# A mixture-of-experts feed-forward: one set of transposes, rows scaled once, routing between the blocks of the shared experts

## The chip, the core and the metric

The kernel runs on one core of one Trainium2 chip. The time is device microseconds (us) of one execution, taken as the median of several runs; the profile is one more execution, recorded by the hardware profiler. The engines have their own instruction queues and work side by side: TensorE (PE, with its weight loads shown apart as PEld), VectorE (DVE), ScalarE (ACT), GpSimd (POOL) and SyncE (SP), which here issues most of the DMA transfers. An engine executes its own instructions in order and waits on semaphores for the others.

## What is computed

A small Perceiver-like network of two layers on x of shape (4, 256, 256): 1024 tokens of 256 features, all in f32. Each block adds to x what it computes from the layer norm of x:

```python
x = x + L0_xattn(layernorm(x), ctx_1024, ctx_1024)
x = x + L0_attn(layernorm(x), pos, ...)
x = x + L0_ffn(layernorm(x), ...)
x = x + L1_xattn(layernorm(x), ctx_1024, mask)
x = x + L1_attn(layernorm(x), ...)
x = x + L1_ffn(layernorm(x), ...)
```

The change is in the third block (and moves some of its loads into the second). With u the normed rows:

```python
def L0_ffn(u, g_shared, W1_s, b1_s, W2_s, b2_s, g_routed, W1_r, b1_r, W2_r, b2_r, centroids):
    # _experts_mlp(x, g, W1, b1, W2, b2): for each expert
    #     gelu((rmsnorm(x) * g) @ W1 + b1) @ W2 + b2        (erf gelu, hidden size 1024)
    h_s = _experts_mlp(u, g_shared, W1_s, b1_s, W2_s, b2_s).sum(axis=-2)   # 2 shared experts
    scores = sigmoid(u @ centroids)                                        # 8 routed experts
    gpk, i_topk = top_k(scores, 2)
    gk = gpk / scores.sum(axis=-1, keepdims=True)
    h_r = weighted sum of the 2 chosen experts' outputs, weights gk
    return u + h_s + h_r
```

So the block's result is x + u + h_s + h_r. The router works on u, the experts on the rows of u divided by their root mean square.

## The kernel before

Tokens lie in 8 tiles of 128 (TT = 8, P = 128), the features in two halves of 128 (DC = 2), the hidden size in 8 parts of 128 (FC = 8). x stays in SBUF as [128, 8, 256]. Matmuls go through `contract` (L169, the matmul itself is L175), so most of them carry one line number in the profile and are told apart by the names of their tiles.

The blocks run one after the other (`BLOCKS`, L1644). `l0_attn` (L549) loads its weights, computes a relative-position attention over the batch axis, and ends with the output projection `ao`: a contraction over two halves and a bias row for each token tile, then an add to x on DVE (L668). Of its loads the ones named here are `a0_wT`, `a0_pT`, `a0_bias` and the row `a0_ob`, which the projection adds.

`l0_ffn` (L772) does the following. Where nothing else is said, the order on each engine is chosen by the tile scheduler from the dependences; the text order below is the program's.

- It loads the centroids and the output biases `f0_b2` (L781, L782), zeroes a DRAM table of rows, `f0_rows` (L785), and loads the first shared expert's weights (two loads of 1 MB, L797 to L803).
- `normed` (L233) computes the layer norm of all eight tiles into u (tile `xn`): statistics, `rsqrt` (twelve small DVE instructions, three Newton steps, L177 to L194), and one DVE instruction for each tile (L247).
- `transposed` (L255) turns u into `uT` by 16 PE transposes (tile `tr`) and four copies out of PSUM. The router's logits `cs` are contractions of `uT` with the centroids (L806 to L812); Exp (L814), a few DVE steps and `top2` (L817) give the chosen experts, the gates follow (L822).
- A second `rsqrt` gives the inverse root mean square r (L824). For each tile POOL adds u to x (L826) and DVE scales u by r (L827). A second set of 16 transposes with four scaled copies makes `sT`, the experts' input (L828).
- `place` (L694) works out where each token's row goes in a table sorted by expert: two matmuls for ranks (L707, L708), a chain of DVE instructions, and one large POOL product, `part` (L765, tile tag `h`), with its reduction (L769) for the biases of the routed tiles. Sixteen indirect DMAs on POOL's queue scatter the rows into `f0_rows` (L830 to L835).
- For each token tile the gates are transposed (`gT`, L839), copied by ACT (L841), multiplied with the biases (L843) and added to x (L844). Below this is the bias block.
- The eight routed experts' weights (16 loads of 1 MB) are issued on SP (L850 to L858).
- The shared experts (L845 to L872): for each of two experts e and each of four blocks n of 256 tokens, first the hidden layer `h`: eight parts f of 128 hidden units, each a contraction over two halves into half of a PSUM bank, and a Gelu from there into the SBUF tile `h` (two buffers). Two parts share a bank tile, and four such tiles rotate (`sc=(4, 1)`). Then the output `eo`: for each of two token tiles a contraction over eight f, and an add to x on DVE (L872).

```python
for f in range(FC):
    if f % 2 == 0:
        sc = self.sc_tile("h")[:, 0, :]
    part = sc[:, f % 2 * 256 : (f % 2 + 1) * 256]
    self.contract(part, [(w1[:, k, f * P : (f + 1) * P], sT[:, k, cols]) for k in range(DC)])
    nc.scalar.activation(h[:, f, :], part, AF.Gelu, bias=self.col("f0_b1", (NE + e) * FC + f))
```

- The routed experts (L873 to L936) work through 23 tiles of sorted rows in an order written out by hand (`manual_schedule`): rows are read back from `f0_rows`, transposed (`rT`), multiplied with the weights of the tile's expert, and written to DRAM; then the rows are gathered back and added to x with their gates (L937 to L946).

Inside `manual_schedule` the scheduler leaves the program's order as it is on every engine. The PSUM pools of the block are `mm_tile` (three banks), `sc_tile` (four) and `ps_o` (one).

Of the kernel before, what the change touches and what calls it, by code (L numbers as in the profile page):

```python
# [74 lines left out]
class Net:  # L75
# [157 lines left out]
    def normed(self, x, out, tiles=range(TT), square=None):  # L233
# [9 lines left out]
        if square is not None:  # L243
            nc.vector.tensor_mul(square, rstd, rstd)
            nc.vector.tensor_mul(square, square, mv[:, :, 1])
# [300 lines left out]
    def l0_attn(self, x):  # L546
# [3 lines left out]
        with ExitStack() as ctx:  # L550
# [6 lines left out]
            nc.sync.dma_start(bias, a["a0_bias"].partition_broadcast(P))  # L557

# [212 lines left out]

    def l0_ffn(self, x):  # L772
# [4 lines left out]
        with ExitStack() as ctx:  # L777
            pool = self.block(ctx, "f0", sc=(4, 1))
            rows = self.tc.dram_tile([SLOT_TILES * P, D], F32, name="f0_rows")
            results = self.tc.dram_tile([SLOT_TILES * P, D], F32, name="f0_results")  # L780
            cent = self.load_w(pool, "f0_cent")  # L781
            b2 = self.load(pool, "f0_b2", [NE + 2, D], a["f0_b2"])  # L782
            zero = pool.tile([P, D], F32, name="f0_zero")
            nc.gpsimd.memset(zero, 0.0)
            nc.sync.dma_start(  # L785
                rows.rearrange("(t p) d -> p t d", p=P), zero.unsqueeze(1).to_broadcast([P, SLOT_TILES, D])
            )
# [3 lines left out]
            ms = self.small.tile([P, TT], F32, tag="ms", name=self.name("ms"))  # L791
            u = self.normed(x, self.tokens("xn"), square=ms)
            w1_all, w2_all = (pool.tile([P, NE, DC * FF], F32, name=f"f0_w{n}_all") for n in (1, 2))
            with self.tc.tile_pool(name="f0_shared", bufs=1, reuse_waits="tile") as first:
                weights = {}

                def shared_weights(e):  # L797
                    weights[e] = (
                        self.load(first, "w1", [P, DC, FF], a["f0_W1_s"][e].rearrange("(k p) n -> p k n", p=P)),
                        self.load(first, "w2", [P, FC, D], a["f0_W2_s"][e].rearrange("(k p) n -> p k n", p=P)),  # L800
                    )

                shared_weights(0)  # L803
                uT = self.transposed(u, "xT", pool=first)
                score = first.tile([P, TT, NE], F32, name="f0_score")
                ps = self.mm_tile("cs")  # L806
                for i in range(TT):
                    self.contract(
                        ps[:, i * NE : (i + 1) * NE], [(uT[:, k, i * P : (i + 1) * P], cent[:, k, :]) for k in range(DC)]
                    )  # L810
# [34 lines left out]
                for e in range(2):  # L845
                    if e:
                        shared_weights(e)
# [799 lines left out]
def build(tc, a, out):  # L1647
    nc = tc.nc
    with ExitStack() as ctx:
# [4 lines left out]
        for block in BLOCKS:  # L1654
            x = getattr(net, block)(x)
# [163 lines left out]
```

## Time and profile before

| what | us |
|---|---|
| runs | 2363.99, 2364.1, 2373.08 |
| median of the runs | 2364.1 |
| the profiled execution | 2370.56 |
| its span in the profile | 2368.8 |
| its mean granted TensorE clock | 0.95 |

By stages, from the windows of the profile (a stretch from the span's start, and the busy time of two engines in it, in us):

| stretch | what runs there | length | PE busy | DVE busy |
|---|---|---|---|---|
| 0 to 270.0 | first cross attention, and the loads of the next blocks | 270.0 | 240.1 | 87.8 |
| 270.0 to 360.3 | `l0_attn` to its last `ao` matmul | 90.3 | 73.4 | 60.7 |
| 360.3 to 402.7 | norm, routing, transposes, bias block, first `h` parts | 42.4 | 30.6 | 32.7 |
| 402.7 to 511.1 | shared experts | 108.4 | 108.4 | 7.4 |
| 511.1 to 697.0 | routed experts | 185.9 | 184.8 | 39.8 |
| 697.0 to 2368.8 | gather, and the three blocks of layer 1 | 1671.8 | 1587.1 | 960.6 |

How to read such a profile: a share of busy time is an average over stages with different limits, so the stage that a change touches is read by itself. A line with "x32" stands for 32 records taken together; a 128x128 by 128x256 matmul in f32 leaves two records, so one part f of an `h` block (two matmuls) leaves four and a whole block 32. "[0.16 <-ACT h L867]" after a line means that the engine stood idle for 0.16 us before it, and that the wait ended with ACT's instruction of line 867 on tile `h`. The granted clock is a share of full speed. SPq is SP's DMA queue.

### The profile page before, as it was taken

What the parts mean: (1) busy time and instruction counts of PE and PEld (TensorE: products, weight loads), DVE (VectorE), ACT (ScalarE), POOL (GpSimd) and SP (SyncE); (2) the same over time, 40 slices, a digit from 0 to 9 for tenths busy, and PEclk for the clock granted to TensorE, in tenths of its full rate; (3) what the DMA queues carried; (4) which work ended last, traced back from release to release, by engine and by line L of the source; (5) the groups of instructions that cost most, each with busy time, mean ns of one, the idle gap of its engine ahead of it and who ended that gap; (6) DMA issues with size and microseconds to landing.
All of it is one profiled execution on the core that took longest, in us unless ns stands there. A gap on an engine that the chain in (4) does not pass through costs nothing.

```text
span 2368.8 us, 45856 instructions
## 1 busy us (share of the span) xinstructions
PE 2224.3 (94%) x19148; PEld 1339.5 (57%) x19148; DVE 1189.0 (50%) x2494; ACT 982.6 (41%) x1942; POOL 146.5 (6%) x270
## 2 busy tenths in 40 slices
PE   6999877999988999999999999999999899999996
PEld 4677535876752454455545554455554566666552
DVE  2333476012215766666666666665665176343545
ACT  0111111223333366655666556655555524344321
POOL 0000002100011000000000000000000042000121
PEclk9999866999999999999999999999999999999977
DMA  6121118101124112211121112210000120000000
GB/s 202 54 89 32 36 51 293 63 16 36 32 87 147 45 39 66 66 31 35 49 64 56 32 34 61 63 46 29 29 7 2 62 78 1 1 1 1 6 0 14
DMA packets 82432, 121.50 MB, mean 51 GB/s; under 512 B 5466, under 2 KB 52338, under 8 KB 82226
## 3 DMA queue, kind: packets, MB, share of 16 engines
q1 hardware_dynamic: 80690, 114.38, 15.4%
q0 software_dynamic: 1536, 4.20, 0.5%
q8 instruction: 151, 2.47, 0.4%
q14 instruction: 55, 0.45, 0.1%
HBM read 109.32 MB, written 9.24 MB: 50 GB/s over the span
## 4 chain that ended last, share of the span: by engine, by line
PE 87%; DVE 6%; issue 3%; ACT 2%; DMA 2%; SPq 0%; POOL 0%; POOLq 0%; DVEq 0%; ACTq 0%
PE sc L1092 14%; PE acc L1143 10%; PE mx L1105 9%; PE h L175 8%; PE v L1000 5%; PE k L1000 5%; PE ro L175 4%; PE we L175 3%; PE gram L414 2%; PE eo L175 2%; PE po L175 2%; PE sc L1560 2%; PE q L175 2%; PE xo L175 1%; PE qkv L175 1%
## 5 line engine op out<-in xcount | busy, mean ns | idle before, releaser
L1134 DVE TENSOR_REDUCE mx<-mx 128x1 f32<-128x512 f32 x988 | 636.6, 686 | 365.0 <-PE mx L1105 361.0
L1130 ACT ACTIVATE probs<-sc 128x512 f32<-128x512 f32 x988 | 536.8, 597 | 422.2 <-PE mx L1105 394.9
L1092 PE MATMUL sc<-qm,kT 32*128 32x256 f32 x3952 | 581.3, 401 | 8.9 <-ACT probs L1130 8.9
L1105 PE MATMUL mx<-kT,x_q 32*128 32x512 f32 x1976 | 561.1, 639 | 0.0
L1092 PEld LDWEIGHTS sc<-qm,kT 32*128 32x128 f32 x3952 | 352.3, 184 | 255.0 <-ACT probs L1130 129.3
L1143 PE MATMUL acc<-probs,v 128*32 128x256 f32 x4096 | 275.6, 386 | 0.0
L1143 PEld LDWEIGHTS acc<-probs,v 128*32 128x32 f32 x4096 | 107.3, 109 | 134.9 <-issue 90.1
L1105 PEld LDWEIGHTS mx<-kT,x_q 32*128 32x128 f32 x1976 | 150.9, 183 | 8.5 <-issue 7.2
L1000 PE MATMUL k<-slab,x_wk 128*32 128x512 f32 x1024 | 136.1, 618 | 11.8 <-DMA slab<-in_ctxT 10.9
L1000 PE MATMUL v<-x_wv,slab 128*32 128x256 f32 x2048 | 137.1, 385 | 0.0
L1574 DVE TENSOR_REDUCE negm<-mx 128x2 f32<-128x512 f32 x128 | 82.7, 686 | 94.8 <-PE mx L1566 92.9
L1572 ACT ACTIVATE probs<-sc 128x512 f32<-128x512 f32 x128 | 69.5, 595 | 136.1 <-PE mx L1566 93.9
L1566 PE MATMUL mx<-k,q 32*128 32x256 f32 x512 | 90.3, 435 | 24.5 <-DVE negm L1574 19.5
L309 ACT ACTIVATE kT<-k,cols 128x512 f32<-128x512 f32 x128 | 92.8, 783 | 23.2 <-PE k L1000 23.2
L346 POOL COPY wide<-rec 128x256 f32<-128x256 f32 x48 | 19.1, 398 | 1328.4 <-DVE rec L344 1317.0
L1000 PEld LDWEIGHTS v<-x_wv,slab 128*32 128x32 f32 x2048 | 53.4, 109 | 74.4 <-issue 46.3
L414 PE MATMUL gram<-x_ctx 128*128 128x257 f32 x256 | 79.2, 391 | 14.3 <-DMA x_ctx<-in_ctx 14.3
L1560 PE MATMUL sc<-qm,k 32*128 32x256 f32 x512 | 88.6, 439 | 0.0
L175 PE MATMUL h<-f_w_all,rT 128*128 x184 | 83.0, 594 | 0.7 <-DVE rT L888 0.6
L175 PE MATMUL ro<-f_w_all,hT 128*128 x368 | 83.3, 379 | 0.1
L912 ACT ACTIVATE hT<-hT,place 128x128 f32<-128x128 f32 x184 | 49.9, 383 | 77.8 <-PE hT L909 77.7
L175 PEld LDWEIGHTS ro<-f_w_all,hT 128*128 128x128 f32 x368 | 68.2, 190 | 9.1 <-issue 0.5
(365 smaller groups left out, 2664.4 us busy)
## 6 DMA issues: line engine op xcount, KB each, us to landing
slab<-in_ctxT SPq DMA_DIRECT2D x96, 512.0 KB
x_ctx<-in_ctx SPq DMA_DIRECT2D x16, 1024.0 KB
f_w_all<-in_f_W_r SPq DMA_DIRECT2D x16, 1024.0 KB
w<-in_f_W_s SPq DMA_DIRECT2D x4, 1024.0 KB
f_rows<-f_zero SPq DMA_DIRECT2D x1, 2944.0 KB
row<-f_rows SPq DMA_DIRECT2D x23, 128.0 KB
f_results<-y SPq DMA_DIRECT2D x23, 128.0 KB
kT<-away SPq DMA_DIRECT2D x128, 8.0 KB
```

The costliest lines, as they stand in the source:

```text
L175: nc.tensor.matmul(out, w, m, start=i == 0, stop=i == len(pairs) - 1)
L309: nc.scalar.activation(dst, ps, AF.Identity, bias=b, scale=own)
L414: nc.tensor.matmul(ps[:, : D + 1], t[:, :P], t, start=n == 0, stop=False)
L1000: nc.tensor.matmul(out[own], w[:, own], m, start=start, stop=not start, tile_position=(0, 32 * j))
L1092: nc.tensor.matmul(into[:, c * S : (c + 1) * S], kT[b, u, at // HALF][rows, at % HALF : at % HALF + P], qm[un][rows, :], start=True, stop= ...
L1105: nc.tensor.matmul(into, q[rows, b, u, t * P : (t + 1) * P], kT[b, u, at // HALF][rows, at % HALF : at % HALF + SLAB], start=True, stop=True,)
L1130: nc.scalar.activation(probs[j], sc[j], AF.Exp, scale=0.25)
L1134: nc.vector.tensor_reduce(mx[un2][:, k2 % 2, j, k2 // 2 : k2 // 2 + 1], bd[j], AX.X, ALU.max)
L1143: nc.tensor.matmul(acc[32 * j : 32 * j + 32, :S], v[b, chunk // VC][:, at : at + 32], probs[j][:, c * S : (c + 1) * S], start=k == 0 and c ...
L1560: nc.tensor.matmul(sc[j][:, c * S : (c + 1) * S], k[key][on_rows(j), u, c * P : (c + 1) * P], qm[i][on_rows(j), :], start=True, stop=True,)
L1566: nc.tensor.matmul(bd[j][:, c * S : (c + 1) * S], q[key][on_rows(j), u, c * P : (c + 1) * P], k[key][on_rows(j), u, :], start=True, stop=True,
L1574: nc.vector.tensor_reduce(negm[i2 % 2][:, :, 32 * j + UNIT_MAX[i2 % 2]], bd[j].rearrange("p (t s) -> p t s", s=S), AX.X, ALU.max, negate=True,
```

## The change

Four things are changed in the third block, and the order of its middle part is written out.

- The loads of the centroids, `f0_b2` and the first shared expert, and the zeroing of `f0_rows` move into `l0_attn`, after its own weight loads (`before_ffn`); their tiles live in a pool that is opened before `l0_attn`.
- The norm is done in two halves, tiles 0, 2, 4, 6 and then 1, 3, 5, 7. Both inverse roots are worked out first, and one DVE instruction for each tile writes u already divided by its root mean square (`by` = rstd times r). One set of transposes feeds both `uT` (plain copy, DVE) and `sT` (scaled by the gain, ACT). The logits of these scaled rows are multiplied back by `back`, which is one over r. x + u is computed by ACT as x times (1 + rstd) plus a shift, in place of POOL's adds.
- The routed experts' loads are issued ahead of the shared experts' first block.
- From Exp on, the order is by hand: `lower` (an `h` block) and `upper` (an `eo` block) alternate, with the gates, `place`, the scatter and the bias block at written places among them. `b2` gets the bank of `ps_o`, `gT` three buffers; the second shared expert is loaded after the first one's last block.

```diff
-    def normed(self, x, out, tiles=range(TT), square=None):
+    def normed(self, x, out, tiles=range(TT)):
...
-        if square is not None:
-            nc.vector.tensor_mul(square, rstd, rstd)
-            nc.vector.tensor_mul(square, square, mv[:, :, 1])
...
             nc.sync.dma_start(bias, a["a0_bias"].partition_broadcast(P))
+            self.before_ffn()
...
+    def before_ffn(self):
+        nc, a = self.nc, self.a
+        self.f0_rows = self.tc.dram_tile([SLOT_TILES * P, D], F32, name="f0_rows")
+        zero = self.early.tile([P, D], F32, name="f0_zero")
+        nc.gpsimd.memset(zero, 0.0)
+        self.f0_cent = self.load_w(self.early, "f0_cent")
+        self.f0_b2 = self.load(self.early, "f0_b2", [NE + 2, D], a["f0_b2"])
+        self.f0_shared = {}
+        self.shared_weights(0)
+        nc.sync.dma_start(
+            self.f0_rows.rearrange("(t p) d -> p t d", p=P), zero.unsqueeze(1).to_broadcast([P, SLOT_TILES, D])
+        )
+    def shared_weights(self, e):
+        a = self.a
+        self.f0_shared[e] = (
+            self.load(self.early, "w1", [P, DC, FF], a["f0_W1_s"][e].rearrange("(k p) n -> p k n", p=P)),
+            self.load(self.early, "w2", [P, FC, D], a["f0_W2_s"][e].rearrange("(k p) n -> p k n", p=P)),
+        )
...
-            ms = self.small.tile([P, TT], F32, tag="ms", name=self.name("ms"))
-            u = self.normed(x, self.tokens("xn"), square=ms)
+
+            back = pool.tile([P, TT], F32, name="f0_back")
...
-                shared_weights(0)
-                uT = self.transposed(u, "xT", pool=first)
+                sT = first.tile([P, DC, NT], F32, name="f0_sT")
+                uT = first.tile([P, DC, NT], F32, tag="h", name="f0_uT", bufs=2)
+                ps_c = self.mm_tile("cs")
+                logit = first.tile([P, TT, NE], F32, name="f0_logit")
+                columns = lambda t, c, half: t.rearrange("p c (t f n) -> p c t f n", f=2, n=P)[:, c, :, half, :]
+                for half in range(2):
+                    tiles = range(half, TT, 2)
+                    n = len(tiles)
+                    new = lambda what, *more: self.small.tile([P, n, *more], F32, tag=what, name=self.name(what))
+                    stats, mv = new("bn", 6), new("mv", 2)
+                    for k, i in enumerate(tiles):
+                        nc.vector.bn_stats(stats[:, k, :], x[:, i, :])
+                        nc.vector.bn_aggr(mv[:, k, :], stats[:, k, :])
+                    rstd = self.rsqrt(mv[:, :, 1], EPS)
+                    ms, by, keep, shift = new("ms"), new("by"), new("keep"), new("shift")
+                    nc.vector.tensor_mul(ms, rstd, rstd)
+                    nc.vector.tensor_mul(ms, ms, mv[:, :, 1])
+                    r = self.rsqrt(ms, EPS_RMS)
+                    nc.vector.tensor_mul(by, rstd, r)
+                    for k, i in enumerate(tiles):
+                        nc.vector.tensor_scalar(
+                            u[:, i, :], x[:, i, :], mv[:, k, 0:1], by[:, k : k + 1], ALU.subtract, ALU.mult
+                        )
+                    nc.vector.scalar_tensor_tensor(back[:, half::2], ms, EPS_RMS, r, op0=ALU.add, op1=ALU.mult)
+                    nc.vector.tensor_scalar(keep, rstd, 1.0, None, ALU.add)
+                    nc.vector.scalar_tensor_tensor(shift, mv[:, :, 0], -1.0, rstd, op0=ALU.mult, op1=ALU.mult)
+                    for c in range(DC):
+                        ps = self.mm_tile("tr")
+                        for k, i in enumerate(tiles):
+                            nc.tensor.transpose(ps[:, k * P : (k + 1) * P], u[:, i, c * P : (c + 1) * P], self.ident)
+                        ps = ps.rearrange("p (t n) -> p t n", n=P)
+                        nc.vector.tensor_copy(columns(uT, c, half), ps)
+                        nc.scalar.activation(columns(sT, c, half), ps, AF.Identity, scale=self.col("f0_gs", c))
+                    for i in tiles:
+                        self.contract(
+                            ps_c[:, i * NE : (i + 1) * NE],
+                            [(uT[:, k, i * P : (i + 1) * P], cent[:, k, :]) for k in range(DC)],
+                        )
+                    for k, i in enumerate(tiles):
+                        nc.scalar.activation(
+                            x[:, i, :], x[:, i, :], AF.Identity, bias=shift[:, k : k + 1], scale=keep[:, k : k + 1]
+                        )
+                nc.vector.tensor_tensor(
+                    logit, ps_c[:, : TT * NE].rearrange("p (t e) -> p t e", e=NE),
+                    back.unsqueeze(2).to_broadcast([P, TT, NE]), ALU.mult,
+                )
...
-                r = self.rsqrt(ms, EPS_RMS)
-                for i in range(TT):
-                    nc.gpsimd.tensor_add(x[:, i, :], x[:, i, :], u[:, i, :])
-                    nc.vector.tensor_scalar(u[:, i, :], u[:, i, :], r[:, i : i + 1], None, ALU.mult)
-                sT = self.transposed(u, "xT", "f0_gs", pool=first)
...
+                hidden = {}
+                def lower(e, n):
+                    w1 = self.f0_shared[e][0]
+                    cols = slice(n * 256, (n + 1) * 256)
+                    h = hidden[e, n] = first.tile([P, FC, 256], F32, tag="h", name=self.name("h"), bufs=2)
+                    for f in range(FC):
+                        if f % 2 == 0:
+                            sc = self.sc_tile("h")[:, 0, :]
+                        part = sc[:, f % 2 * 256 : (f % 2 + 1) * 256]
+                        self.contract(part, [(w1[:, k, f * P : (f + 1) * P], sT[:, k, cols]) for k in range(DC)])
+                        nc.scalar.activation(h[:, f, :], part, AF.Gelu, bias=self.col("f0_b1", (NE + e) * FC + f))
+                def upper(e, n):
+                    w2, h = self.f0_shared[e][1], hidden.pop((e, n))
+                    for q in range(2):
+                        i = 2 * n + q
+                        ps = self.mm_tile("eo")
+                        self.contract(ps[:, :D], [(h[:, f, q * P : (q + 1) * P], w2[:, f, :]) for f in range(FC)])
+                        nc.vector.tensor_add(x[:, i, :], ps[:, :D], x[:, i, :])
+                with self.tc.manual_schedule():
+                    nc.scalar.activation(score, logit, AF.Exp, scale=-1.0)
+                    lower(0, 0)
+                    nc.vector.tensor_scalar(score, score, 1.0, None, ALU.add)
+                    nc.vector.reciprocal(score, score)
+                    nc.vector.tensor_copy(chosen, self.top2(score, logit, first))
+                    nc.vector.tensor_reduce(total, score, AX.X, ALU.add)
+                    nc.vector.reciprocal(total, total)
+                    nc.vector.tensor_mul(score, score, chosen)
+                    nc.vector.tensor_mul(gates[:, :, :NE], score, total.unsqueeze(2).to_broadcast([P, TT, NE]))
+                    lower(0, 1)
+                    upper(0, 0)
+                    lower(0, 2)
+                    slots, shares, where, bias = self.place(first, pool, chosen, gates[:, :, :NE])
+                    upper(0, 1)
+                    for side in range(2):
+                        for i in range(TT):
+                            nc.gpsimd.indirect_dma_start(
+                                out=rows, out_offset=bass.IndirectOffsetOnAxis(ap=slots[:, side, i : i + 1], axis=0),
+                                in_=u[:, i, :], in_offset=None,
+                            )
+                    upper(0, 2)
+                    lower(0, 3)
+                    upper(0, 3)
+                    self.shared_weights(1)
                     for i in range(TT):
+                        ps = self.mm_tile("gT")
+                        nc.tensor.transpose(ps[: NE + 2, :P], gates[:, i, :], self.ident)
+                        gT = self.small.tile([NE + 2, P], F32, tag="gT", name=self.name("gT"), bufs=3)
+                        nc.scalar.copy(gT, ps[: NE + 2, :P])
+                        ps = self.ps_o.tile([P, 512], F32, tag="o", name=self.name("b2"))
+                        nc.tensor.matmul(ps[:, :D], gT, b2, start=True, stop=True)
+                        nc.vector.tensor_add(x[:, i, :], ps[:, :D], x[:, i, :])
+                    lower(1, 0)
                     for n in range(4):
+                        if n < 3:
+                            lower(1, n + 1)
+                        upper(1, n)
...
-        for block in BLOCKS:
-            x = getattr(net, block)(x)
+        x = net.l0_xattn(x)
+        with ExitStack() as ffn:
+            net.early = ffn.enter_context(tc.tile_pool(name="f0_early", bufs=1, reuse_waits="tile"))
+            x = net.l0_attn(x)
+            x = net.l0_ffn(x)
```

The lines of top two, gates, `place` and the loads of the routed weights are the same as before, apart from their place.

## Prediction

> **What bounds the kernel now.** I read the page from the top (busy time, clock, the chain that ended last), then stage windows, and then the chain and the timeline of the one stage that the change rewrites.
>
> ```profile
> span 2368.8 us, 45856 instructions
> PE 2224.3 (94%) x19148; PEld 1339.5 (57%) x19148; DVE 1189.0 (50%) x2494; ACT 982.6 (41%) x1942; POOL 146.5 (6%) x270
> ...
> PE 87%; DVE 6%; issue 3%; ACT 2%; DMA 2%; SPq 0%; POOL 0%; POOLq 0%; DVEq 0%; ACTq 0%
> ```
>
> TensorE sets the end. Work taken from another engine gains only where PE stands and waits for it. The windows (span's stretch, its length, then busy time of PE, PEld, DVE, ACT, POOL, the granted clock, DMA share, GB/s) show where that is:
>
> ```profile
> 360.30:402.70 42.40, 30.56 (x111) 20.54 (x111) 32.66 (x109) 6.18 (x16) 11.66 (x11) 0.60 1.02 363
> 402.70:511.10 108.40, 108.40 (x494) 93.55 (x495) 7.43 (x17) 28.40 (x60) 13.79 (x15) 0.99 0.17 57
> ```
>
> From the last `ao` matmul (360.3) on, PE waits for norms and routing, at a clock of 0.60. From 402.7 the shared experts run with PE busy for 108.40 of 108.40 us at 0.99. The chain of waits:
>
> ```profile
> 364.40 4.87 DVE xn L247 x7
> ...
> 370.64 6.64 PE cs L175 x32
> ...
> 383.08 3.90 PE tr L263 x16
> ...
> 407.50 6.91 PE eo L175 x32
> 414.40 6.91 PE h L175 x32
> ```
>
> One 256-token half of an expert layer is one block of 32 records: 6.92 us, whether `h` or `eo`, so 1.73 us for each of the four bank tiles of an `h` block, 0.865 for each of a tile's two f parts. Sixteen blocks make 16 x 6.92 = 110.7 us. The routed stage begins at 511.1, so the experts began as if at 511.1 - 110.7 = 400.4, with the bias work (L839 to L844) between the first `h` parts. The timeline of one `h` block shows the hand-over between TensorE and the Gelu:
>
> ```profile
> 455.52 1.70 PEld L175 LDWEIGHTS h<-xT,w 128*128 128x128 f32 x8
> 455.74 7.10 PE L175 MATMUL h<-xT,w 128*128 128x256 f32 x32
> ...
> 456.86 0.47 ACT L867 ACTIVATE h<-h,cols 128x256 f32<-128x256 f32 x1 [7.36 <-PE h L175]
> 457.39 5.04 PEld L175 LDWEIGHTS h<-xT,w 128*128 128x128 f32 x24 [0.16 <-ACT h L867]
> ```
>
> Eight loads are two parts (four records each). The third part's load then waits for the Gelu of the first, 456.86 + 0.47 = 457.33, and starts 0.06 later, 1.65 after the block's first matmul. The first two parts' matmuls last until 455.74 + 1.73 = 457.47, so today the wait is just covered.
>
> **The change, part by part.** All is counted from 360.3, where the last `ao` matmul ends in both.
>
> *Removed and hidden.* The 16 second transposes (3.90 above), their four scaled evacuations, eight POOL adds and eight scales L827 go. Eight ACTIVATEs (`keep`) come; by the 0.595 us of a 128x256 ACTIVATE they take 4.8 us on ACT beside DVE's norm. The loads moved ahead (`f0_cent`, `f0_b2`, `w1`, `w2`, the zeroing) go on SP in front of `a0_ob`, which is first needed at 336, and were landed at 259 already; POOL's memset comes before `bias`, which waits 204 us for its DMA. I cost them at nothing; if that cover failed, `ao` at 336 would start late by what is missing. The routed weights keep their start (after the last `ao`) and their queue; the second shared set, each half of it 1 MB that arrived within some 6 us before (449 to 455 and 456 to 461), is issued after the last reader of the first (`lower(0, 3)`, `upper(0, 3)`) and has the bias block and more to arrive in. The row scatter (POOL) starts after `part`, about 431 by the sum below, and 16 x 2.67 us (one start to the next, 413.51 to 416.18) ends at 474; it is needed at the routed stage, 60 us later. Instructions from the routed stage on are the same.
>
> *Front.* In the built program's instruction order the first half's small operations stand between the adds of the last four `ao` tiles. DVE then needs 2.07 to 2.27 us per tile (add 0.44, statistics 0.44 + 0.19, five or six small ones of 0.2) where `ao` tiles come every 1.68: the last add starts 1.35 late, at 361.65. It, four small ones and the last statistics reach 363.5; four `xn` of 0.33 follow with transposes behind them (eight of 0.25 at half clock), two `uT` copies of 0.68: 367.3. The second half's chain stands after these: 26 small ones of 0.2 = 5.2, to 372.5; four `xn` 1.3; transposes and `uT`, to 375.4; seven `cs` contractions of 0.43: 378.4; logit and Exp 0.9, to 379.3; the table load for Gelu (1.28, now behind Exp) and the first Gelu: 381.2, when PE goes on with tile 0's second part. A tile up to there costs 1.65, so the experts begin as if at 379.6: **-20.8 us**. Bounds: 376 (no backlog) to 383.
>
> *The wait inside a tile.* Now the order is by hand: `lower` writes part 0, its Gelu, part 1, its Gelu. In the built program part 1's first matmul waits, in all 32 bank tiles, for the Gelu of part 0 of the same tile: four tiles rotate, but each is guarded as a whole. Before, the scheduler had put another tile's part 0 between (the eight loads above). PE issues in order; the next tile's part 0, `eo` and the rank matmuls are queued behind. A tile becomes 1.65 (first matmul to part 1's load), 0.11 for that load with nothing over it (512.04 to 512.15 at the routed stage's first `h`, where the load after two starts at 512.58, one matmul of 0.43 later), and 0.865: 2.625 against 1.73. 32 x 0.895 = **+28.6**. Bounds: 1.60 (the block of 414.24 has its first Gelu after 1.07, not 1.12) and no load, 0.735, to 1.65 with a whole load of 0.21 (455.52 to 455.74), 0.995: 23.5 to 31.8.
>
> *Bias block.* `gT`, its copy, `b2` were laid between `h` parts and are now alone, PE waiting for ACT each time: 0.27 + 0.06 + 0.25 + 0.06 + 0.62 = 1.26 per token tile (389.10 to 390.36); at half clock a cycle took 1.92 (397.73 to 399.65). 8 x 1.26 = 10.1 to 15.4; half cold, **+12.7**.
>
> *Stall in `upper(0, 2)`.* `part` takes a buffer of `h` and so waits for `upper(0, 1)`. Then POOL 3.91, the reduce 1.67, and behind it on DVE the add (0.42) that frees the bank of `upper(0, 2)`'s second `eo`: 6.1 after `upper(0, 1)`, where PE is ready after 3.46. **+2.7** (0 to 4.4). The two rank matmuls, now in PE's order between blocks, took 0.32 + 0.43 (L707, L708); bare loads and a bank to wait for bring it to **+1.2** (0.75 to 1.5).
>
> *Clock.* `cs` and the bias block keep PE partly idle, and such stretches were granted half:
>
> ```profile
> 396.00:400.00 4.00, 3.60 (x8) 1.17 (x6) 3.56 (x9) 1.91 (x4) 3.55 (x2) 0.50 1.05 380
> ...
> 720.00:725.00 5.00, 3.30 (x32) 0.69 (x23) 1.79 (x6) 3.19 (x5) 3.48 (x8) 1.00 0.92 280
> 725.00:730.00 5.00, 3.46 (x32) 0.99 (x32) 1.49 (x4) 2.31 (x4) 0.47 (x5) 1.00 0.97 347
> ```
>
> The clock changed in steps of some 3.4 us, so after each of the two stretches one to two of them run cold. A tile takes 4.46 then (worked out at the rivals) against 2.625: 1.5 x 3.4 x (1 - 2.625 / 4.46) = 2.1, twice: **+4.2** (0 to 5.6, two steps each). Within `lower`, PE works 1.73 of 2.625 us, 66%; the last two rows are 66% and 69% and kept the full clock. I take no throttling there.
>
> A rule speaks against that: the Trainium skill, "TensorE: Matmul & The Clock Gate", section "A second HAM failure mode: psum-queue depth-cycling", says that micro-idles between groups of matmuls, with PSUM banks cycled, make the clock swing between half and full. By it the lowers would be the throttled rival below; by the two rows at 720 and 725 they are not, and the rows decide my sum.
>
> **Sum.** -20.8 + 28.6 + 12.7 + 2.7 + 1.2 + 4.2 = +28.6 us: the routed stage starts at 540. The profiled execution (2370.6, its span and 1.8 around it) would become 2399; it lay 6.5 over the median of the runs, and from that, 2364.1, the time is **2393**. All lower bounds (376, 23.5, 10.1, 0, 0.75, 0) give +10, all upper ones (383, 31.8, 15.4, 4.4, 1.5, 5.6) +41: 2374 to 2405.
>
> **The rivals.** *The clock stays at half in the lowers.* For: 0.50 at 396 to 400 with gaps of the same kind. Against: 720 to 730. At half clock both parts and a bare load double: 1.73 + 0.25 + 0.47 + 0.06 + 0.22 + 1.73 = 4.46, 1.84 more. The first two lowers cold: 8 x 1.84 less the step counted = +12.6, 2405; the same again after the bias block, 2418; all 32, 2393 + 58.9 - 4.2 = 2448. Chance 0.14.
>
> *The pause in the tile is not there (not slower).* If PE gets on with part 1 under the Gelu after all, the 28.6 fall away and the rest is 0: 2364; with the bias block warm and neither stall nor cold steps (-9.5) 2355. For: today 32 tiles run without a gap. Against: the row at 457.39, where one part fewer ahead of it would already have left PE idle, and the new order. It decides below a pause of 0.37 us per tile (11.8 us in all); between 0.37 and 0.6 the loss is small. Chance 0.13.
>
> *A transfer is late.* A half of the second shared set that nothing covers costs its 6 us: 2399. For: it can't be issued before the last reader of the first set, as now. Against: 12.7 us of that block and `upper(0, 3)`, 6.9, lie between. Chance 0.05. *The routing stays exposed as now*, so that the front's 20.8 isn't got: 2414; `cs` and what precedes it would have to take 40 us with half the transposes gone. Chance 0.02.
>
> **How the numbers follow.** My forecast has 0.66: 2393, its own range 2383 to 2401. This kernel tells a change from none from about 0.5% on, 11.8 us. Below 2352.3 only the no-pause rival with some further luck comes: faster 0.04; up to 2375.9 most of that rival and the low end of mine: same 0.12; slower 0.84. The range leaves out most of the no-pause rival and the colder half of the clock's: 2377 to 2409.
>
> **What would show it.** Right: 32 gaps of about 0.75 us on PE's weight loads, released by the Gelu's ACT, and `h` blocks of about 10.5 us against `eo` blocks of 6.9; Exp near 379; a bias block of 10 to 15 us on its own; the scatter over by about 475; the first `rT` matmul near 540; a span near 2397. Wrong: `h` blocks of 6.9 us; a granted clock of 0.5 in lowers after the first; `h` of expert 1 waiting for `w`; gaps at the routed stage for `f_rows`; or a difference that arises outside 360 to 540.

## The result, and the profile after

The changed kernel is slower: 2405.26 us, the median of four runs (2394.86 to 2406.04), against 2368.59 for the kernel before (four runs, 2363.99 to 2379.55). The ratio is 1.013, with a 95% interval of 1.0108 to 1.0152. That is 26 to 36 us. The ratios given here and below are those on record; the plain quotients of the medians differ from them by up to 0.0025 (here it is 1.0155), which changes no sign. One of e1's ten runs took 3581.77 us at a mean clock of 0.55 and is left out of its ratio.

The page of the changed kernel begins like this (busy time by engine, then the chain that ended last by engine):

```profile
span 2403.7 us, 45844 instructions
PE 2243.3 (93%) x19132; PEld 1345.3 (56%) x19132; DVE 1189.7 (49%) x2518; ACT 989.0 (41%) x1952; POOL 140.5 (6%) x262
...
PE 86%; DVE 6%; issue 3%; ACT 2%; DMA 2%; SPq 0%; POOL 0%; POOLq 0%; DVEq 0%; ACTq 0%
```

It has 16 PE instructions fewer, and PE is busy 19.0 us longer: busy time contains the half clock, at which the same eight records of `h` take 3.78 us and not 1.99 (both below). Where the time went shows only by stages. I measured each profile between two marks that all kernels share, the last `ao` record and the first `rT` matmul (from start to start):

| kernel | `ao` | `rT` | between | `rT` to the end |
|---|---|---|---|---|
| before | 359.9 | 511.1 | 151.2 | 1857.7 |
| changed | 357.2 | 537.3 | 180.1 | 1866.4 |

So 28.9 us of the loss lie in the rewritten stage and 8.7 behind it; the last `ao` came 2.7 earlier, which leaves the 34.9 by which the spans differ. Its windows (stretch, length, busy time of PE, PEld, DVE, ACT, POOL, granted clock, DMA share, GB/s) are the front, the first `h` block up to its fourth tile, warm tiles of `h`, and the bias block:

```profile
360.00:376.00 16.00, 12.90 (x51) 10.70 (x49) 9.54 (x43) 7.48 (x14) 0.00 (x0) 0.50 1.06 379
376.80:389.80 13.00, 11.32 (x24) 7.54 (x24) 3.80 (x11) 2.84 (x6) 0.00 (x0) 0.51 1.05 378
389.80:400.00 10.20, 7.98 (x32) 5.76 (x32) 0.00 (x0) 3.79 (x8) 0.00 (x0) 1.00 1.07 377
...
452.90:465.80 12.90, 9.76 (x25) 3.75 (x23) 3.40 (x8) 2.03 (x8) 3.83 (x4) 0.69 0.34 112
```

In none of these stretches is PE always busy, as it was in the kernel before from 402.7 to 511.1. The timeline shows the same tile at half clock and, from 389.81 on, at full clock:

```profile
381.12 3.78 PE L175 MATMUL h<-f_sT,w 128*128 128x256 f32 x8 [0.56 <-ACT h L878]
...
385.47 3.78 PE L175 MATMUL h<-f_sT,w 128*128 128x256 f32 x8 [0.56 <-ACT h L878]
...
389.81 1.99 PE L175 MATMUL h<-f_sT,w 128*128 128x256 f32 x8 [0.56 <-ACT h L878]
390.98 0.47 ACT L878 ACTIVATE h<-h,cols 128x256 f32<-128x256 f32 x1 [1.22 <-PE h L175]
391.85 0.47 ACT L878 ACTIVATE h<-h,cols 128x256 f32<-128x256 f32 x1 [0.39 <-PE h L175]
392.37 1.59 PEld L175 LDWEIGHTS h<-f_sT,w 128*128 128x128 f32 x8 [0.96 <-ACT h L878]
392.37 1.99 PE L175 MATMUL h<-f_sT,w 128*128 128x256 f32 x8 [0.56 <-ACT h L878]
```

Eight matmul records are part 1 of one tile and part 0 of the next. Then PE stands, and what ends the wait is ACT's Gelu of the part 0 just made (391.85 + 0.47 = 392.32, and PE goes on at 392.37). A tile takes 392.37 - 389.81 = 2.56 us, and 385.47 - 381.12 = 4.35 at half clock; before, it took 1.73.

### The profile page after: what moved, and what is told of

The parts are those of the page before. It is cut to its first block, busy times and chain, and to the rows that moved or that the text cites. A ratio compares the mean times of both kernels' runs of the same rounds, so it can differ in the third digit from the quotient of the medians.

```text
span 2403.7 us, 45844 instructions
## 1 busy us (share of the span) xinstructions
PE 2243.3 (93%) x19132; PEld 1345.3 (56%) x19132; DVE 1189.7 (49%) x2518; ACT 989.0 (41%) x1952; POOL 140.5 (6%) x262
## 4 chain that ended last, share of the span: by engine, by line
PE 86%; DVE 6%; issue 3%; ACT 2%; DMA 2%; SPq 0%; POOL 0%; POOLq 0%; DVEq 0%; ACTq 0%
PE sc L1147 14%; PE acc L1198 10%; PE h L175 9%; PE mx L1160 8%; PE v L1055 5%; PE k L1055 5%; PE ro L175 4%; PE we L175 2%; PE gram L411 2%; PE po L175 2%; PE sc L1615 2%; PE eo L175 2%; PE q L175 2%; PE xo L175 1%; PE qkv L175 1%
## 5 line engine op out<-in xcount | busy, mean ns | idle before, releaser
L1621 PE MATMUL mx<-k,q 32*128 32x256 f32 x512 | 96.3, 459 | 24.8 <-DVE negm L1629 19.5
L1615 PE MATMUL sc<-qm,k 32*128 32x256 f32 x512 | 93.5, 462 | 0.0
L175 PE MATMUL h<-f_sT,w 128*128 128x256 f32 x256 | 74.0, 433 | 19.4 <-ACT h L878 19.3
```

What stands on the lines that cost most here:

```text
L175: nc.tensor.matmul(out, w, m, start=i == 0, stop=i == len(pairs) - 1)
L1615: nc.tensor.matmul(sc[j][:, c * S : (c + 1) * S], k[key][on_rows(j), u, c * P : (c + 1) * P], qm[i][on_rows(j), :], start=True, stop=True,)
L1621: nc.tensor.matmul(bd[j][:, c * S : (c + 1) * S], q[key][on_rows(j), u, c * P : (c + 1) * P], k[key][on_rows(j), u, :], start=True, stop=True,
```

## The experiments

"From `ao` to `rT`" is by the marks of the table; the expectations count from the end of the last `ao` matmul, which gives 0.6 less. Ratios are to the kernel before. e6, e8, e9 and e12 were run once each, so only the stages of their profiles are compared. The stage repeats well: e12, the changed kernel again, gives the same 180.1.

**e1: the wait inside the tile, taken away.**

```diff
-for f in range(FC):
-    if f % 2 == 0:
-        sc = self.sc_tile("h")[:, 0, :]
-    part = ...
-    self.contract(part, ...)
-    nc.scalar.activation(h[:, f, :], part, AF.Gelu, ...)
+for f in range(0, FC, 2):
+    sc = self.sc_tile("h")[:, 0, :]
+    for j in range(2):
+        self.contract(parts[j], ...)
+    for j in range(2):
+        nc.scalar.activation(h[:, f + j, :], parts[j], AF.Gelu, ...)
```

> The changed kernel, with lower() writing both parts of a bank tile before the two Gelus. From the last ao matmul to the first rT matmul the kernel before took 150.6 us and the changed one 179.5. My theory (the wait inside the tile costs 32 x 0.83 = 26.6): h blocks of 6.9 us without gaps, 150 to 153 us from ao to rT, a time within 0.4% of the kernel before. Rival 'the clock' (the loss lies in the half-clock stretches, the gaps only go with them): the stretches at half clock up to 390 and from 457 to 471 stay as long, and less than 10 us come back. Rival 'a transfer or the scatter sets the start of the routed stage': h blocks of 6.9 us, but PE then stands in front of rT or the routed h, and the 179.5 hardly move.

Measured: 147.6 us from `ao` to `rT`, 32.5 less than the changed kernel, and a time of 0.9992 of the kernel before (0.9973 to 1.0012). The timeline has the first `h` block and the next in one piece:

```profile
375.17 16.10 PE L175 MATMUL h<-f_sT,w 128*128 128x256 f32 x62
...
391.10 7.07 PE L175 MATMUL eo<-w,h 128*128 128x256 f32 x32
```

62 records in 16.10 us with no wait in front of them; later blocks take 6.9. The routed stage starts that much earlier, so no transfer holds it. More came back than the 26.6 of the waits: the full clock, too, came 10 us sooner: at 380.2, 22.1 after the last `ao` mark, where the changed kernel had it at 389.5, 32.3 after (more on this at e6).

**e2: the order by hand, taken away.**

```diff
-with self.tc.manual_schedule():
+if True:
     nc.scalar.activation(score, logit, AF.Exp, scale=-1.0)
     lower(0, 0)
     ...
```

> The changed kernel without the order written by hand: the scheduler orders shared experts, place, scatter and bias block as it did before, all else (early loads, halves, one set of transposes) stays. My theory: only the front's gain is left (22.5 us, part of it lost again to a cold clock at the start), 128 to 138 us from ao to rT, 0.5 to 0.9% faster than the kernel before. Rival 'the front's gain is not real, the early routing only moves the wait': 150 or more. Rival 'a transfer or the scatter sets the start of the routed stage': PE stands before the routed stage by what is missing to 150.

Measured: 137.6 us, and 0.9953 of the kernel before (0.9933 to 0.9972). The front's gain is real, and the scheduler covers the wait by itself: an `h` block again takes 7.10 us without a gap, as at 455.74 in the kernel before. That another tile's part 0 again stands ahead of part 1 is inferred from this.

```profile
398.55 7.10 PE L175 MATMUL h<-f_sT,w 128*128 128x256 f32 x32
```

The gain in time, 0.47% (0.28 to 0.67), is just short of the 0.5 to 0.9 that I expected.

**e3: the wait, put into the kernel before.** The loops over shared experts and blocks keep their written order; nothing else changes.

```diff
-for e in range(2):
-    ...
+with self.tc.manual_schedule():
+    for e in range(2):
+        ...
```

> The kernel before, with the loops of the shared experts kept in their written order (part, Gelu, part, Gelu, then eo), nothing else changed. My theory: 32 tiles of 2.56 in place of 1.73, 150.6 + 26.6 = 177 us from ao to rT, 1.1% slower. Rival 'the clock': partly busy h blocks fall to half clock, 4.35 us per tile, 200 us or more. Rival 'the loss of the changed kernel comes from its other edits': under 160.

Measured: 185.0 us, +33.8, and a ratio of 1.0165 (1.014 to 1.019). The wait makes the kernel before at least as slow as the whole change did, without any of its other parts. It is 7 more than I expected. Of these, 5.4 are three tiles of the first block at half clock, 3 x (4.35 - 2.56); the later blocks had the full one. The other 2 were not taken apart; the bias block lost the `h` parts between its matmuls here too.

```profile
402.30:414.90 12.60, 11.34 (x24) 7.57 (x24) 2.38 (x4) 2.42 (x6) 4.23 (x5) 0.50 0.38 127
424.80:433.30 8.50, 6.76 (x28) 5.02 (x29) 0.00 (x0) 2.85 (x6) 3.17 (x4) 1.00 0.14 48
```

(The windows of e3's first `h` block and of its second.)

**e4: the bias block, folded into `eo`.**

```diff
+gT = first.tile([NE + 2, NT], F32, name="f0_gT")
 ...
-self.contract(ps[:, :D], [(h[:, f, ...], w2[:, f, :]) for f in range(FC)])
+pairs = [(h[:, f, ...], w2[:, f, :]) for f in range(FC)]
+if e:
+    pairs.append((gT[:, i * P : (i + 1) * P], b2))
+self.contract(ps[:, :D], pairs)
```

The eight transposes of the gates go into two banks ahead of `lower(0, 3)`, with two copies; the old block is dropped.

> The changed kernel, its bias block taken apart: eight transposes of the gates into two banks with two copies ahead of lower(0, 3), and the biases as a ninth matmul in each contraction of the second expert's eo. The order by hand and the wait inside the tiles stay. My theory: the block's 13.0 us and the cold tiles behind it (2.5 to 4) go, 8 x 0.43 + 8 x 0.27 = 5.6 come: 167 to 171 us from ao to rT, 9 to 12 us faster than the changed kernel. Rival 'the block only fills time in which the second expert's weights arrive': PE then waits for w at expert 1, and nothing is gained.

Measured: 171.8 us, 8.3 less than the changed kernel and so short of the 9 to 12 expected; a ratio of 1.0106 (1.0086 to 1.0126), where the changed one has 1.013. PE had no wait for the second expert's weights. A folded bias costs more than the 0.43 I gave it: from one contraction's start to the next it was 4.28 us (518.36 to 522.64) in place of 3.46.

```profile
518.36 3.72 PE L175 MATMUL eo<-w,h 128*128 128x256 f32 x16
...
522.01 0.69 PE L175 MATMUL eo<-f_b,f_gT 10*128 10x256 f32 x2
...
522.64 3.72 PE L175 MATMUL eo<-w,h 128*128 128x256 f32 x16
```

**e5: three edits together.** Those of e1 and e4, and the product `part` with its reduction (`place_bias`, cut out of `place`) after `upper(0, 1)`.

```diff
 slots, shares, where, bias, rest = self.place(...)
 upper(0, 1)
+self.place_bias(*rest, bias)
```

> Three edits of the changed kernel together: both parts of a tile before their Gelus, the biases folded into eo, and the reduction of part issued after upper(0, 1). From e1's 147.6 us (last ao to first rT matmul): less 12.9 of bias block and 1.6 of half clock behind it, less 3.0 of stall in upper(0, 2), plus the 7.6 that the folded biases took in e4: 137 to 139 us, 0.4 to 0.6% faster than the kernel before. Rival 'the order of the scheduler is what gains, not these terms': 143 or more.

Measured: 139.1 us, and 0.9938 (0.9915 to 0.9961): faster than the kernel before and the changed one. PE still stood 1.3 us between 415 and 435, which e8 explains.

**e6: the pairs of e1 in `lower(0, 0)` alone.**

```diff
+if (e, n) == (0, 0):
+    ...
+    return
 for f in range(FC):
     ...
```

> The changed kernel with the two parts ahead of their Gelus in lower(0, 0) alone; the other seven h blocks keep the wait. My theory of the clock (a full PE gets the clock back in one or two steps and the later blocks, 66% busy, keep it, where the gaps of lower(0, 0) kept it at half for 13 us): 4 x 0.83 of waits, 1.6 at the first tile, and 3.5 of half clock less, 171 to 173 us from ao to rT; full clock from about 381 on. Rival 'gaps only, the clock comes back by its own time': half clock up to 390 as before, 175. Rival 'the next block with gaps falls back to half': 178 or more.

Measured: 172.6 us. The last `ao` mark lay at 353.1 in this profile and the clock was full from 375.0 on, 21.9 later, as in e1. One block without gaps brings the clock back 10 us sooner (in the five profiles with gaps in that block, those of the changed kernel, e4, e8, e9 and e12, it came 32.3 after the mark), and the blocks with gaps behind it keep it, at 2.56 per tile, up to the bias block.

**e7: the moved loads alone, in the kernel before.**

```diff
 nc.sync.dma_start(bias, a["a0_bias"].partition_broadcast(P))
+self.before_ffn()
```

> The kernel before with the moved loads alone (centroids, biases, first shared expert, zeroing of the rows go into the attention block). My theory: nothing on the path waits for them in either place, 151 us from ao to rT, time within 0.3% of the kernel before. Rival 'they hold up the attention's own loads': the last ao matmul later than 361, or a wait of ao for its row. Rival 'they gain': ao to rT under 148.

Measured: 151.2 us from `ao` to `rT`, the same as before; last `ao` at 358.6; a ratio of 1.0007 (0.9987 to 1.0027). They cost and gain nothing.

**e8: the stall, first try.** The changed kernel with `part` and its reduction after `upper(0, 1)`, so that DVE has the adds of that block first; the diff is that of e5.

> The changed kernel with part and its reduction issued after upper(0, 1), nothing else. My theory: the adds of upper(0, 1) are no longer behind the reduction on DVE, the 3.0 us stall of upper(0, 2) goes, 177 us from ao to rT. Rival 'the stall only moves to the next eo': 179.5 to 180.5, with PE waiting for DVE in upper(0, 2) or upper(0, 3).

Measured: 179.8 us, so the expectation failed. The timeline says why:

```profile
426.60 3.93 POOL L769 TENSOR_TENSOR part<-place,cols 128x1472 f32<-128x1472 f32 x1 [105.87 <-DVE place L752]
426.67 3.90 DVE L758 CAST place<-place 128x23 int32<-128x23 f32 x1
430.49 0.74 DVE L890 TENSOR_TENSOR x<-eo,x 128x256 f32<-128x256 f32 x2
...
430.95 2.43 PE L175 MATMUL eo<-w,h 128*128 128x256 f32 x10 [1.32 <-DVE x L890]
```

The adds do stand ahead of the reduction now. But the instruction in front of them, a cast of 23 numbers in each partition, began 0.07 us after POOL's product and ended with it: 3.90 us. The stall fell from 3.0 to 1.3, and 1.4 of that went to one more step of half clock behind the bias block (17.1 us at half there, 13.7 in the changed kernel).

**e9: the stall, second try.** `part`, its reduction and the scatter are issued after `lower(0, 3)`; POOL's product then runs beside matmuls of `h`, when DVE has no adds.

```diff
 upper(0, 1)
 upper(0, 2)
 lower(0, 3)
+self.place_bias(*rest, bias)
+for side in range(2):
+    ...
 upper(0, 3)
```

> The changed kernel with part, its reduction and the scatter issued after lower(0, 3), so that POOL's product runs beside an h block, where DVE has no adds. In e8 a cast of 23 numbers on DVE (L758) took 3.9 us and ended with POOL's part. My theory now (DVE was held while POOL's product ran, whatever stood in its queue): the cast, now long before part, takes 0.2 us, the stall of upper(0, 2) is gone (under 0.5), 176 to 178.5 us from ao to rT, the rest being one clock step more or less. Rival 'the cast is slow by itself': it takes 3.9 us again, and 1.3 us or more of the stall stay.

Measured: the cast took 0.18 us, and the stall was gone: the four contractions of `upper(0, 1)` and `upper(0, 2)` follow each other, 64 records in 14.03 us.

```profile
420.47 14.03 PE L175 MATMUL eo<-w,h 128*128 128x256 f32 x64
...
428.09 0.18 DVE L758 CAST place<-place 128x23 int32<-128x23 f32 x1
...
434.64 3.94 POOL L769 TENSOR_TENSOR part<-place,cols 128x1472 f32<-128x1472 f32 x1 [112.57 <-PE eo L175]
```

From `ao` to `rT`, though, it was 180.6 us and not 177. The clock gave the 3.0 back: behind the bias block it stayed at half through all of `lower(1, 0)`, 23.9 us in all for 13.7, so that three tiles took 4.35, where the changed kernel lost 2.4 us there and this one 6.4.

**e10: e5 with `part` and the scatter placed as in e9** (the diffs of e1, e4 and e9).

> As e5 (pairs, folded biases), with part, its reduction and the scatter placed as in e9. My theory: the 1.3 us for which PE still stood between 415 and 435 in e5 go: 137 to 138.5 us from ao to rT, 0.5 to 0.7% faster than the kernel before. Rival 'the later scatter is now late': PE waits in front of the routed stage.

Measured: 137.5 us, 2353.97 us (2352.00 to 2359.55) and 0.9914 of the kernel before (0.9893 to 0.9935), the lowest of all, though its interval overlaps that of e5 and just touches that of e2. In the stage it is level with e2 (137.6); in the two profiles the difference lies behind the stage (1861.1 from `rT` to the end, and 1864.5 in e2). The windows of e10:

```profile
375.00:395.00 20.00, 20.00 (x82) 17.33 (x83) 5.82 (x15) 8.26 (x18) 0.00 (x0) 0.85 1.06 375
395.00:415.00 20.00, 20.00 (x97) 17.65 (x96) 8.20 (x40) 3.36 (x8) 0.00 (x0) 1.00 0.53 187
415.00:435.00 20.00, 20.00 (x98) 17.46 (x97) 3.18 (x5) 4.41 (x10) 7.07 (x4) 1.00 0.21 73
```

PE is busy for all of these 60 us, and with no bias block the clock, once up, stays up.

**e11: e2 with the folded biases** (the diffs of e2 and e4).

> As e2 (no order by hand), with the biases folded into eo. In e2 all beyond front, 16 blocks, ranks and cold start comes to about 6 us, the folded biases took 7.6 in e4: my theory is no gain, 137 to 140 us from ao to rT. Rival 'the scheduler hides folded biases better': 134 or less.

Measured: 138.1 us, 0.995 (0.9928 to 0.9972). Nothing is gained over e2. Presumably the scheduler hides the bias block between `h` parts about as cheaply as the folded one costs; that was not taken apart.

**e12: the changed kernel once more**, unchanged.

> The changed kernel once more, for what lies behind the routed stage, where no instruction was changed: so far the part from the first rT matmul to the end took 1857.7 us before, 1866.4 in the changed kernel, and 1856.5 to 1875.1 in the experiments. My theory (where the clock's steps fall in partly busy stretches differs from execution to execution): from ao to rT 178.5 to 181.5 again, the part behind it anywhere from 1856 to 1876. Rival 'the change itself makes the rest longer': 1866 again within 1.

Measured: 180.1 us from `ao` to `rT`, and 1866.4 from there to the end. The rival's number came, not a new draw, so my theory of what lies behind the stage isn't supported. What can be said: that part has the same instructions in all the kernels and took 1856.5 us in e8 (which differs from the changed kernel in two places before it) and 1875.1 in e1; the two profiles of the changed kernel agree within 0.1. Where they differ from the kernel before, the clock differs: 0.85 for 100 us from the first `ro` scale on (1915.0) against 0.91 for the same stretch of the kernel before (from 1890.8 on). In e8, too, it was 0.91. (The kernel before, then the changed one.)

```profile
1890.80:1990.80 100.00, 89.71 (x654) 61.66 (x654) 70.09 (x197) 29.79 (x60) 37.79 (x56) 0.91 0.19 63
...
1915.00:2015.00 100.00, 89.70 (x613) 60.43 (x614) 68.07 (x193) 29.75 (x59) 33.97 (x51) 0.85 0.19 63
```

Whether the length of the changed stage decides at which step of the clock that part begins, or whether the two profiles agree by chance, stays open; one run of the changed kernel (2394.86) was 10 to 11 us shorter than the other three.

## Why the prediction was right, and where it was off

The forecast was 2393 (2377 to 2409); measured were 2405.26, and by the ratio +31 on the kernel before. That is inside the range, but above the 2383 to 2401 that I gave my own sum. In the stage itself +28.6 was forecast, and +28.9 is what the profiles show. Term by term:

| term | forecast | measured | from |
|---|---|---|---|
| front | -20.8 | -22.6 | PE goes on with part 1 of tile 0 at 376.77, 19.2 after the last `ao` ended (357.58); less 1.65 is 17.5, before 40.1 |
| wait inside a tile | +28.6 | +26.6 | 32 x (2.56 - 1.73) |
| bias block | +12.7 | +13.0 | 452.9 to 465.85 |
| stall in `upper(0, 2)` | +2.7 | +3.0 | the idle 2.99 in front of its second `eo` |
| rank matmuls | +1.2 | +0.6 | 418.00 to 418.61 |
| half clock | +4.2 | +7.8 | 3 x (4.35 - 2.56) in `lower(0, 0)`, 2.4 in `lower(1, 0)` |
| sum | +28.6 | +28.4 | 28.9 in the table of marks |

The rows of the changed kernel behind the front and the stall:

```profile
376.77 3.78 PE L175 MATMUL h<-f_sT,w 128*128 128x256 f32 x8 [1.34 <-ACT h L878]
...
426.16 3.91 POOL L763 TENSOR_TENSOR part<-place,cols 128x1472 f32<-128x1472 f32 x1 [105.84 <-DVE place L752]
426.23 3.88 DVE L758 CAST place<-place 128x23 int32<-128x23 f32 x1
430.10 1.69 DVE L767 TENSOR_REDUCE place<-part 128x184 f32<-128x1472 f32 x1
...
432.18 3.72 PE L175 MATMUL eo<-w,h 128*128 128x256 f32 x16 [2.99 <-DVE x L886]
```

That the sums agree within 0.3 is in part luck: the front and the wait came out 1.8 and 2.0 lower than forecast, the half clock 3.6 higher.

*The main step held.* Part 1 waits for the Gelu of part 0 in its own tile, nothing in PE's order covers the wait, and the pause sets the pace: shown both ways, by taking it out of the changed kernel (e1) and by putting it into the kernel before (e3). The weight load with nothing over it was sized too high: 2.56 leaves little over 1.65 + 0.865 = 2.515.

*Front.* The gain was 1.8 larger. A small DVE instruction behind a long one starts before that ends (an add at 355.93, the small one at 356.27, though the add takes 0.42), and two adds stood 1.69 apart (355.93 to 357.62), the pace of the `ao` tiles. The backlog of 1.35 that I counted was not there.

*Bias block and stall* came as worked out (the stall's terms as written, 6.1 - 3.46, give 2.6 and not 2.7). The stall's cause was only half seen: I named the reduction in front of the adds; e8 shows that the cast ahead of both was held for all of POOL's product, and that moving the reduction is not enough.

*The clock is the term that was mis-sized.* I let each cold stretch last one and a half steps of 3.4 us. Behind the bias block of the changed kernel it lasted 5.5 us (465.85 to 471.37), about as I had it. In `lower(0, 0)` it lasted for three whole tiles, 13.0 us, and 12.6 in e3. At half clock a tile with the wait has PE busy for 3.78 of 4.35 us, 87%, and that did not bring the clock back for nearly four steps; without gaps, in e1, it came 5.0 us after the matmuls had begun to run on (375.17 to 380.18).

The mean of 87% hides what decides. The clock changed only at steps of 3.41 us: in the changed kernel at 358.73, 389.45, 457.72 and 471.37, which lie 9, 20 and 4 steps apart. Here are the last three steps at half clock in `lower(0, 0)` and the first at full:

```profile
379.21:382.63 3.42, 2.86 (x8) 1.78 (x7) 1.49 (x7) 0.62 (x2) 0.00 (x0) 0.50 1.09 379
382.63:386.04 3.41, 2.85 (x7) 1.78 (x6) 0.00 (x0) 0.95 (x2) 0.00 (x0) 0.50 1.05 364
386.04:389.45 3.41, 3.21 (x8) 2.02 (x6) 0.00 (x0) 0.64 (x2) 0.00 (x0) 0.50 1.05 390
389.45:392.87 3.42, 2.49 (x10) 1.91 (x11) 0.00 (x0) 1.26 (x3) 0.00 (x0) 1.00 1.10 367
```

The first two hold a whole gap of 0.56 (PE busy for 83.5% of them), the third holds only a part of one (94%), and then the clock is full. I took all steps of the fourteen profiles between `ao` and `rT` that have nothing but `h` and `eo` matmuls of 128 rows. Of those at half clock, 20 were followed by half clock, with PE busy for 71 to 83.5%, and 17 by the full one, with 83.5 to 100% (16 of them 84.6% or more). All 428 at full clock kept it, at 45 to 100%. A cold tile takes 4.35 us and a step 3.41, so a step without a whole gap comes only now and then, and the cold blocks waited for it; by this, how many tiles run cold (three in `lower(0, 0)` and in e9's `lower(1, 0)`, little more than one behind the bias block of the changed kernel) depends on where the gaps fall in the steps. This is worked out from the profiles; no run tested it. It does not carry over to other matmuls: in the kernel before, the `ao` matmuls, a third of them with one row, left PE no idle time in these two steps, and the clock stayed at half:

```profile
337.64:341.05 3.41, 3.41 (x8) 1.93 (x7) 3.34 (x4) 0.00 (x0) 0.00 (x0) 0.50 0.00 0
341.05:344.47 3.42, 3.42 (x8) 1.72 (x7) 3.28 (x6) 0.00 (x0) 0.00 (x0) 0.50 0.00 0
```

The rival "the clock stays at half in the lowers" had this mechanism right for three tiles of the first block, and for three of `lower(1, 0)` in e9, and wrong beyond: at full clock the same blocks, with PE busy for 78% (1.99 of 2.56 us a tile; the 66% that I had put beside the rows at 720 to 730 counts the matmuls' own length), kept it, at 1.00 from 389.8 on in the window above and in all later blocks up to the bias block. Its 2405 for two cold lowers is the measured time by chance: it counted 8 x 1.84 = 14.7 us for the first stretch, where 5.4 were measured. The rows at 720 to 730 answered the question I put to them (is the full clock kept?), and not the other one (is it regained?).

The rule that I had weighed, from the Trainium skill, "TensorE: Matmul & The Clock Gate" ("A second HAM failure mode: psum-queue depth-cycling"), says that such micro-idles make the clock swing to and fro. Here it did not swing in the warm blocks; it came late in the cold ones. The same page ("What's actually happening") has the clock rise after one busy window of some 3.4 us. In e1 the step from 376.77 to 380.18 was such a window, 100% busy, and the clock was full at its end. Busy in the profile's sense is not enough, though: the `ao` steps above were 100% busy too.

*The rivals.* "The pause is not there" is out by every `h` block of the changed kernel. "A transfer is late" is out: PE never waited for `w` or `f_rows` there, and e1 started the routed stage 32.5 earlier with the same transfers. "The routing stays exposed" is out by e2.

*The rest of the difference.* The time is 12 above the forecast, for the most part for two reasons outside the stage. The median that I started from, 2364.1, lies 6.5 below the profiled execution, at the low end of what this kernel showed since (2363.99 to 2387.34 in 47 runs). And the part behind the routed stage took 8.7 longer in the profile of the changed kernel, with the same instructions (e12). Less the 2.7 by which the last `ao` came earlier, the two make 12.5; why the part behind took longer stays open.

## What to carry to other kernels

When an order is written out by hand, write the producer of all parts of a buffer before the first consumer: a guard holds the whole tile, and whatever order the scheduler had found to cover it is lost with the scheduler (26.6 us here, for two loops in the wrong order). Ask of a pause not only what it lasts but what clock PE has when it comes: gaps that a warm PE bears can hold a cold one at half clock (2.56 against 4.35 us a tile), and a saving of 3 us can vanish in a cold start further on (e9). And leave to the scheduler what it does well: the same edits without the order by hand were already faster than the kernel before (e2), and the best order by hand was no shorter in the stage (137.5 us in e10, 137.6 in e2).

## What the runs showed of the hardware

- A short DVE instruction can be held by POOL. A cast of 23 numbers in each partition took 3.88 us in the changed kernel and 3.90 in e8, ending with POOL's product in both, and 0.18 in e9, where POOL was idle; in the kernel before a DVE instruction of the same size took 3.26 and ended at 401.43, 0.04 after `part`. The Trainium skill, "SBUF — State Buffer" ("Who interferes with whom"), describes it: some DVE instructions and GpSimd share a pair of ports, and whoever comes first has it for its whole instruction. The numbers agree. Not all of DVE is held: beside the same product an add with one input in PSUM took its usual 0.42. What costs is that such an add stands behind the cast in DVE's order.

```profile
397.48 3.91 POOL L765 TENSOR_TENSOR part<-place,cols 128x1472 f32<-128x1472 f32 x1 [0.45 <-DVE place L754]
...
397.83 0.42 DVE L844 TENSOR_TENSOR x<-b,x 128x256 f32<-128x256 f32 x1 [0.44 <-PE b L843]
398.17 3.26 DVE L758 TENSOR_SCALAR place<-place 128x23 f32<-128x23 f32 x1
```

- The clock has a memory. In `h` blocks at full clock a PE that is 78% busy keeps it; at half clock one that is 87% busy on the mean did not raise it for some 13 us, until a step of 3.41 us held less than a whole gap.
- A bias of ten rows added as a ninth matmul to a contraction of eight costs 0.82 us (4.28 in place of 3.46, e4), not one matmul's share of 0.43.
